# Moving the exponential ahead of a top-16 search, and cutting an MLP's second sum in two, in a four-layer transformer kernel

## The chip, the cores and the metric

The kernel runs on one core of a Trainium2 chip, as one program with one launch. The metric is the device time of the execution in microseconds (us); smaller is better. Engines are named as in the profile: PE (TensorE, matmul), DVE (VectorE), ACT (ScalarE), POOL (GpSimd) and SP (SyncE, which issues the DMAs).

## The reference

The input x has 128 sequences of 64 tokens with 128 features, in fp32; a context of the same shape and one condition vector per sequence come with it. Four layers follow each other, all with 16 heads of 8 features:

```python
x = L0(x)   # x + cross-attention(norm(x), norm(context))
x = L1(x)   # self-attention, cross-attention, GELU MLP; each with a residual
x = L2(x)   # self-attention, top-16 cross-attention, SwiGLU MLP
x = L3(x)   # self-attention, cross-attention, GELU MLP
```

The norms are scaled and shifted, and most residuals gated, by vectors made from the condition. The attention that the change touches is the second one of L2. There each query looks at 64 keys, and only the 16 with the greatest scores enter the softmax:

```python
scores = jnp.einsum('bqhd,bkhd->bhqk', q, k) / jnp.sqrt(jnp.float32(D))
top_s, top_i = jax.lax.top_k(scores, TOPK)          # TOPK = 16 of 64
attn = jax.nn.softmax(top_s, axis=-1)
vg = jnp.take_along_axis(v_bh[:, :, None, :, :], top_i[..., None], axis=3)
o = jnp.einsum('bhqk,bhqkd->bqhd', attn, vg)
```

In all there are 128 x 16 x 64 = 131072 such rows of 64 scores. Each MLP goes from 128 features to 512 and back; its second matmul is a sum over 4 blocks of 128.

## The kernel before

**Chunks and lanes.** The work is cut in 16 chunks of 8 sequences, that is 512 tokens; a chunk goes through all four layers before its result is stored. `network(LANES, False, acc)` runs eight lanes: eight chunks are in flight at once, each on a lane, and a lane takes the next chunk when its own is nearly written out.

**The order is planned while the program is built.** Every step is handed to `op(engine, cost, outs, ins, give, ...)`, with a cost in ns. `Plan.run` keeps a list of the lanes' next steps (a window of 80 for each), and takes again and again the one that could start earliest by its costs; this order is then the order of the instructions on each engine. `LUCK` is a tuple of 21 numbers, one for each 350 choices, which shift the costs by up to 1% and so break ties. Buffers are planned too: three PSUM tiles "mm" for projections and sums, two "ps" for scores, one "po", 30 SBUF tiles "some", and so on. Ahead of a PE step that the plan expects to idle for more than 1 us, `warm` (L1221) puts matmuls without use that fill half of the idle time.

**Attention.** `attention` makes k (L761, copied by ACT at L763), q (L767, copied with its bias at L770), spread over four row groups by four DMAs (L774), and v (L785, L792). Heads and sequences are then done in two "quads" of four sequences.

- In the plain attentions `weigh` makes the scores transposed (L819), ACT takes the exponential straight out of PSUM (L830), and no maximum is subtracted.
- In the top-16 attention `weigh_rows` makes the scores with queries on partitions (L849), one PSUM tile of 128 x 1024 for each of four steps. Each half of it (8 rows of 64 on each partition) is copied out by ACT (L867). DVE searches it, row by row: the 8 greatest (L887), these replaced by a very small number (L889), the next 8 greatest (L891). L902 then makes a mask of ones and zeros, `score >= 16th greatest`, and sums it up on its way, as `accum_out`, into `counts`. ACT takes the exponential of the scores (L909), POOL multiplies by the mask (L917), PE transposes (L925) and ACT copies to the probability tile (L934).
- `gather` multiplies with the values (L949), where two more columns of ones give the sums of the softmax; ACT copies the result (L959), and it is spilled to DRAM (L960). Sums and values are read back (L977, L981), DVE takes the reciprocal (L984), which is written (L986) and read back spread (L990), and POOL scales (L994). `project` (L1059) and `residual` (L1042, or L1046 and L1047 with a gate) end the attention.

**Norm and MLP.** A norm is L706 on DVE, L719 and L720 on POOL, L727 on DVE, a transpose on PE (L694), and scale and shift at L738 (DVE) and L739 (POOL), or a copy at L748. The MLPs are `gelu_mlp` and `swiglu_mlp` (first products at L1081), and end in `mlp_out`: 16 matmuls into one PSUM tile (L1072), 4 for each of 4 blocks of columns, given to the plan as one step.

**The guard.** Along with each attention POOL adds the reciprocals, the softmax sums and `counts` into three accumulators (L1007, L1008, L1012). After the last chunk these are compared with bounds, and the counts with an exact number; where one partition fails, a second network runs:

```python
nc.vector.tensor_scalar(ok[:, 8 * NH :], acc[2], float(8 * TOPK * nchunk), None, ALU.is_equal)
...
with tc.If(rows_ok < P):
    network(1, True)
```

This "safe" network does all 16 chunks over from the input, with one lane and few buffers (one for q, two for probabilities, ten "some"). All its attentions go through `weigh_rows`; in the plain ones DVE takes each row's maximum from PSUM (L870) and subtracts it (L871) ahead of the exponential, and in the top-16 one the 16 greatest are marked by two replacements, by place, and not by a comparison.

Of the kernel before, what the change touches and what calls it, by code (L numbers as in the profile page):

```python
# [10 lines left out]
AF = mybir.ActivationFunctionType  # L11
# [10 lines left out]
NT = T // P  # L22
# [4 lines left out]
LANES = 8  # L27
NJ = MLP // P
LUCK = (
    47423, 97277, 61821, 98454, 87219, 72030, 46625, 79421, 30261, 36474, 64224,  # L30
    16425, 63569, 65745, 68055, 16097, 89257, 63092, 89779, 79691, 72039,
)
NSOME = 30
NQBD, NPROB, NVAL = 3, 8, 4
SCALE = 1.0 / math.sqrt(HD)
# [64 lines left out]
PE, DVE, ACT, POOL, SP, LATER = "PE", "DVE", "ACT", "POOL", "SP", "LATER"  # L100
# [31 lines left out]
class Plan:  # L132
# [46 lines left out]
    def op(self, engine, cost, outs, ins, give, latency=0.0, bulk=False, table=None, small=0, within=False, port=False, moves=None, rate=1.0, code=4):  # L179
        tiles = list(dict.fromkeys([*outs, *ins]))  # L180
        needs = {}
        for t in tiles:
            if t.writer is not None:
                needs[t.writer] = True
        for t in outs:
            needs.update(dict.fromkeys(t.readers))
        o = Operation(engine, cost, latency, tiles, needs, give, bulk, table, small, within, port)
        o.moves, o.rate, o.code = moves, rate, small or code
        self.count += 1
        o.serial = self.count  # L190
        o.ev = 0 if engine == PE or any(t.kind in self.PSUM for t in tiles) else 1
        for t in outs:
            t.writer, t.readers = o, []
        for t in ins:
            if t not in outs:
                t.readers.append(o)
        for t in tiles:
            t.ops.append(o)
        self.ops.append(o)
# [180 lines left out]
def kernel(ctx: ExitStack, tc: tile.TileContext, ins: dict, out: bass.AP, nchunk: int = NCHUNK):  # L380
    nc = tc.nc
# [261 lines left out]
    def lane(n, plan, work, safe, acc, pieces, vblocks, queries, pool, spills):  # L643
# [4 lines left out]
        op = plan.op  # L648

        def of(*names):  # L650

            return [t for name in names for t in pieces.get(name, ())]

        def sb(shape, tag, bufs=1):
            name = f"{tag}{n}"
            return plan.tile(lambda: work.tile(shape, F32, tag=name, name=name, bufs=bufs), name, bufs)

        def mm(name):
            return plan.tile(lambda: mm_tile(name), "mm")
# [5 lines left out]
        def some(shape):  # L665


            def make():
                a = pool[t.slot]
                return a.rearrange("p (a b) -> p a b", a=shape[1]) if len(shape) == 3 else (  # L670
                    a.rearrange("p (a b c) -> p a b c", a=shape[1], b=shape[2]) if len(shape) == 4 else a
                )

            t = plan.tile(make, "some")
            return t
# [77 lines left out]
        def attention(hq, hkv, wq, bq, wk, wv, made, topk=False):  # L753
# [82 lines left out]
            def weigh_rows(i, prs):  # L836

                quad, gp = divmod(i, 2)
                psc = plan.tile(lambda: ps_s.tile([P, 2, 2, 2, 2, S], F32, tag="ps", name="ps"), "ps")
# [20 lines left out]
                for half in range(2):  # L860
                    ex = some([P, 8, S])

                    def s8(half=half):
                        return psc().rearrange("p g u k b s -> p (g u k b) s")[:, 8 * half : 8 * half + 8]

                    if topk:
                        op(ACT, 585, [ex], [psc], lambda ex=ex, s8=s8: nc.scalar.copy(ex(), s8()))  # L867
                    else:
                        mx = sb([P, 8], "mx", 2)
                        op(DVE, 680, [mx], [psc], lambda mx=mx, s8=s8: nc.vector.tensor_reduce(mx(), s8(), AX.X, ALU.max))  # L870
                        op(DVE, 680, [ex], [psc, mx], lambda ex=ex, mx=mx, s8=s8: nc.vector.tensor_tensor(  # L871
                            ex(), s8(), mx().unsqueeze(2).to_broadcast([P, 8, S]), ALU.subtract
                        ))
                    exs.append(ex)
# [31 lines left out]
                            ), port=True)  # L906
                        ws.append(w)
                for half, ex in enumerate(exs):
                    op(ACT, 570, [ex], [ex], lambda ex=ex: nc.scalar.activation(ex(), ex(), AF.Exp, scale=SCALE), table="exp")  # L909
                    if topk:  # L910
                        w = ws[half]
                        if safe:
                            op(DVE, 690, [ex], [ex, w], lambda ex=ex, w=w: nc.vector.scalar_tensor_tensor(
                                ex(), w(), GONE, ex(), ALU.is_equal, ALU.mult
                            ))
                        else:
                            op(POOL, 1255, [ex], [ex, w], lambda ex=ex, w=w: nc.gpsimd.tensor_tensor(  # L917
                                ex(), ex(), w(), ALU.mult
                            ), port=True)
# [45 lines left out]
            for quad in range(2):  # L965
                if topk or safe:
                    prs = probs()
                    for gp in range(2):
                        weigh_rows(2 * quad + gp, prs)
                else:  # L970
                    prs = weigh(quad)
                gather(quad, prs)
# [67 lines left out]
        def residual(py, x, gate, c, behind):  # L1040
            if isinstance(gate, str):
                op(DVE, 670, [x], [x, py], lambda: nc.vector.tensor_tensor(x(), v3(py()), x(), ALU.add))  # L1042
            else:
                g = by_token(gate, 0, c, [behind])
                y = some([P, NT, D])
                op(DVE, 650, [y], [py, g], lambda: nc.vector.tensor_tensor(y(), v3(py()), g(), ALU.mult))  # L1046
                op(POOL, 1255, [x], [x, y], lambda: nc.gpsimd.tensor_tensor(x(), x(), y(), ALU.add), port=True)  # L1047
# [16 lines left out]
        def mlp_out(gs, w2, x, gate, c):  # L1064

            py = mm("py")

            def sum_up():
                for t in range(NT):
                    cols = slice(t * P, (t + 1) * P)  # L1070
                    for j in range(NJ):
                        nc.tensor.matmul(  # L1072
                            py()[:, cols], lhsT=gs[j // 2]()[:, j % 2, cols], rhs=W[w2][:, j, :], start=(j == 0), stop=(j == NJ - 1)
                        )

            op(PE, 3610, [py], [*gs, *of(w2)], sum_up, code=4 * NT * NJ)
            residual(py, x, gate, c, gs[1])

        def product(w, j, h, name, *takes):
# [6 lines left out]
        def gelu_mlp(h, w1, b1, w2, x, gate, c):  # L1086
            gs = [shared([P, NJ // 2, T], "prob") for _ in range(2)]

            def part(j):
                ph = product(w1, j, h, "ph", *([] if j else gs))  # L1090
                op(ACT, 690, [gs[j // 2]], [ph, *of("biases")], lambda: nc.scalar.activation(
                    gs[j // 2]()[:, j % 2, :], ph(), AF.Gelu_apprx_tanh, bias=bvec(b1, j)
                ), table="gelu")

            for j in range(NJ):
                part(j)
            mlp_out(gs, w2, x, gate, c)

        def swiglu_mlp(h, w1, b1, w2, x, gate, c):

            gs = [shared([P, NJ // 2, T], "prob") for _ in range(2)]

            def part(j):
                pa = product(w1, j, h, "pa", *([] if j else gs))
                z = some([P, T])
                op(ACT, 690, [z], [pa], lambda: nc.scalar.activation(
                    z(), pa(), AF.Silu, bias=bvec(b1, j)
                ), table="silu")
                pg = product(w1, NJ + j, h, "pg")
                op(DVE, 740, [gs[j // 2]], [pg, z], lambda: nc.vector.scalar_tensor_tensor(  # L1110
                    gs[j // 2]()[:, j % 2, :], pg(), bvec(b1, NJ + j), z(), ALU.add, ALU.mult
                ))

            for j in range(NJ):
                part(j)
            mlp_out(gs, w2, x, gate, c)
# [187 lines left out]
```

## Time and profile before

| | |
|---|---|
| median of the runs | 1746.65 us (three: 1745.80, 1746.65, 1761.59) |
| the profiled execution, its own time | 1752.81 us |
| its span, first to last instruction | 1751.0 us |
| mean granted PE clock | 0.979 |
| instructions | 74746 |
| DMA, mean | 149 GB/s, 260.86 MB |

The page has the busy time of each engine and its share of the span, then groups of instructions by line: count, busy time, mean ns of one, and the idle time of the engine ahead of them with what ended it. In a timeline each line is the start and the length in us, the engine, the line of the kernel, the tiles written and read, and in brackets the idle time before it and who ended it. "PEld" is the loading of weights for a matmul. Line numbers are those of the kernel before.

### The profile page before, as it was taken

Reading aid. Unit: us, or ns where it says so; the run is one execution under the profiler, and the core shown is the slowest. Engines: PE = TensorE matmul, PEld = TensorE weight load, DVE = VectorE, ACT = ScalarE, POOL = GpSimd, SP = SyncE. Lnnn points to the kernel's source line nnn. Section 1 sums busy time; section 2 is a strip of 40 time slices with the busy share of each in tenths; the row PEclk is TensorE's granted clock in tenths of the full one; section 3 lists DMA queues with packets and bytes.
Section 4 is the critical chain, followed back from the end, with each engine's and each line's share of the span. In section 5 each row is a group of like instructions: output and inputs, shape, how many; then the busy total and the mean of one; then the engine's idle time right before and its main releaser. Section 6 shows DMA issues by size and latency. Waiting matters only on the chain. (4 is left out here: it accounts for less than half of the span.)

```text
span 1751.0 us, 74746 instructions
## 1 busy us (share of the span) xinstructions
PE 1624.2 (93%) x30425; PEld 1138.2 (65%) x30425; DVE 1248.4 (71%) x6009; ACT 1272.1 (73%) x1806; POOL 1117.3 (64%) x1306
## 2 busy tenths in 40 slices
PE   8977999988899999999998999999998999999998
PEld 5655667666566566766766666677676756666665
DVE  7532545699998976694578379399989899985323
ACT  3745777867587686788687859879887668686762
POOL 8642656666566757675766485586868566666444
PEclk9988999999999999999999999999999899999999
DMA  7576655543334456545654645755454325356343
GB/s 215 164 231 178 189 169 160 158 120 112 92 118 137 115 150 193 147 137 151 171 161 129 184 130 143 211 147 158 125 175 128 98 77 177 108 153 187 118 144 99
DMA packets 296821, 260.86 MB, mean 149 GB/s; under 512 B 53196, under 2 KB 216212, under 8 KB 296468
## 3 DMA queue, kind: packets, MB, share of 16 engines
q1 hardware_dynamic: 296468, 255.99, 50.2%
q8 instruction: 242, 3.96, 1.0%
q14 instruction: 111, 0.91, 0.2%
HBM read 154.83 MB, written 79.04 MB: 134 GB/s over the span
## 5 line engine op out<-in xcount | busy, mean ns | idle before, releaser
L830 ACT ACTIVATE prob<-ps 128x1024 f32<-128x1024 f32 x384 | 376.5, 1025 | 115.1 <-PE ps L819 112.7
L949 PEld LDWEIGHTS po<-prob,vbuf 128*32 128x32 f32 x14336 | 216.1, 111 | 89.1 <-issue 41.0
L949 PE MATMUL po<-prob,vbuf 128*32 128x64 f32 x14336 | 255.9, 223 | 9.6 <-issue 5.1
L727 DVE TENSOR_SCALAR some<-x,parts,rstd 128x128 f32<-128x128 f32 x640 | 212.4, 393 | 65.0 <-POOL rstd L720 64.8
L819 PE MATMUL ps<-qbd,some 32*64 32x256 f32 x6144 | 226.8, 393 | 18.8 <-DMA qbd<-some 14.1
L917 POOL TENSOR_TENSOR some<-some,some 128x512 f32<-128x512 f32 x128 | 163.6, 1286 | 102.7 <-ACT some L909 66.8
L720 POOL TENSOR_TENSOR rstd<-rstd,minus_half 128x4 f32<-128x4 f32 x192 | 199.0, 1037 | 16.0
L889 DVE MATCH_REPLACE8 some<-m,some 128x64 f32<-128x64 f32 x1024 | 206.4, 209 | 0.3 <-issue 0.3
L1047 POOL TENSOR_TENSOR x<-x,some 128x512 f32<-128x512 f32 x112 | 142.8, 1278 | 81.4 <-DVE some L1046 51.2
L994 POOL TENSOR_TENSOR some<-some,some 128x512 f32<-128x512 f32 x112 | 143.4, 1281 | 80.1 <-DMA some<-spillrec 20.9
L959 ACT COPY some<-po 128x512 f32<-128x512 f32 x224 | 132.6, 592 | 77.9 <-PE po L949 64.9
L887 DVE MAX8 m<-some 128x8 f32<-128x64 f32 x1024 | 172.1, 209 | 15.9 <-ACT some L867 15.9
L891 DVE MAX8 m<-some 128x8 f32<-128x64 f32 x1024 | 176.9, 214 | 0.0
L819 PEld LDWEIGHTS ps<-qbd,some 32*64 32x64 f32 x6144 | 119.7, 133 | 83.8 <-issue 41.0
L792 ACT COPY vbuf<-pv 64x512 f32<-64x512 f32 x224 | 154.2, 688 | 27.4 <-PE pv L785 25.3
L739 POOL TENSOR_TENSOR some<-some,mod_L 128x512 f32<-128x512 f32 x112 | 116.7, 1044 | 84.3 <-DVE some L738 62.5
L1038 POOL TENSOR_TENSOR x<-x,some 128x512 f32<-128x512 f32 x112 | 142.9, 1278 | 42.8 <-DVE some L727 26.5
L1046 DVE TENSOR_TENSOR some<-py,some 128x512 f32<-128x512 f32 x112 | 76.1, 683 | 115.8 <-PE py L1059 63.2
L706 DVE BATCH_NORM_STATS2 parts<-x 128x6 f32<-128x256 f32 x320 | 119.7, 418 | 34.9 <-POOL x L1047 34.0
L694 PE MATMUL pn<-ident,some 128*128 128x128 f32 x768 | 122.0, 283 | 7.2 <-DVE some L727 4.7
L694 PEld LDWEIGHTS pn<-ident,some 128*128 128x128 f32 x768 | 89.2, 142 | 51.1 <-issue 16.7
L763 ACT COPY some<-pk 128x512 f32<-128x512 f32 x112 | 66.3, 593 | 57.4 <-PE pk L761 46.5
(202 smaller groups left out, 3252.4 us busy)
## 6 DMA issues: line engine op xcount, KB each, us to landing
spill<-some SPq DMA_DIRECT2D x224, 256.0 KB, 3.4
some<-gates SPq DMA_DIRECT2D x224, 256.0 KB, 3.7
qbd<-some SPq DMA_DIRECT2D x448, 64.0 KB, 2.4
some<-spill SPq DMA_DIRECT2D x112, 256.0 KB, 4.0
some<-spillrec SPq DMA_DIRECT2D x112, 256.0 KB, 4.5
some<-in_ctx_dram SPq DMA_DIRECT2D x48, 256.0 KB, 5.1
gates<-once SPq DMA_DIRECT2D x7, 1024.0 KB, 7.4
x<-in_x_dram SPq DMA_DIRECT2D x16, 256.0 KB, 4.5
```

Of the source, the lines that this page charges most:

```text
L694: nc.tensor.transpose(p()[:, t * P : (t + 1) * P], x()[:, t, :], ident)
L720: nc.gpsimd.tensor_tensor(rstd(), rstd(), minus_half, ALU.pow)
L727: nc.vector.tensor_scalar(xn()[:, t, :], x()[:, t, :], mv()[:, t, 1:2], rstd()[:, t : t + 1], ALU.subtract, ALU.mult)
L792: nc.scalar.copy(v4(vbuf())[rows, :, :, 0 : 2 * HD].rearrange("p m h (d b) -> p m h d b", b=2)[:, :, :, :, b], pv()[rows].rearrange("p (m ...
L819: nc.tensor.matmul(pscs[g // 2]()[b * S : (b + 1) * S, g % 2, u].rearrange("p (h q) -> p h q", h=4), lhsT=kT()[rows, cols], rhs=qbd()[rows ...
L830: op(ACT, 975, [pr], [psc], lambda pr=pr, psc=psc: nc.scalar.activation(pr().rearrange("p g u h q -> p (g u h q)"), psc().rearrange("p g u ...
L887: nc.vector.max(m1()[:, j, :], ex()[:, j, :])
L889: nc.vector.match_replace(w()[:, j, :], m1()[:, j, :], ex()[:, j, :], GONE)
L891: nc.vector.max(m2()[:, j, :], w()[:, j, :])
L917: op(POOL, 1255, [ex], [ex, w], lambda ex=ex, w=w: nc.gpsimd.tensor_tensor(ex(), ex(), w(), ALU.mult), port=True)
L949: nc.tensor.matmul(po()[32 * j : 32 * j + 32, g, u], lhsT=vbuf()[:, at : at + 32], rhs=prs[gp]()[:, gi, u, j], start=True, stop=True,)
L994: nc.gpsimd.tensor_tensor(oT().rearrange("p (t b q) -> p b t q", b=2, q=S), oS().rearrange("p (b t q) -> p b t q", b=2, q=S), rb().rearran ...
```

## The change

In the fast network's top-16 attention, ACT no longer copies the scores out of PSUM but writes their exponentials, scaled by 1/sqrt(8) as before. The search, the mask and the counts work on these exponentials, and the exponential after the search goes. The safe network keeps its copy and its later exponential. The second sum of the MLPs is given to the plan as two steps of two column blocks each, the second of which may be taken as soon as the first is (`within`). `LUCK` has other numbers, and so the whole order is planned anew. Nothing else is different; the guard is the same.

```diff
 LUCK = (
-    47423, 97277, 61821, 98454, 87219, 72030, 46625, 79421, 30261, 36474, 64224,
...
+    69399, 87246, 10362, 72724, 8023, 6195, 73002, 47238, 78098, 36278, 14865,
...
                     if topk:
-                        op(ACT, 585, [ex], [psc], lambda ex=ex, s8=s8: nc.scalar.copy(ex(), s8()))
+                        if safe:
+                            op(ACT, 585, [ex], [psc], lambda ex=ex, s8=s8: nc.scalar.copy(ex(), s8()))
+                        else:
+                            op(ACT, 585, [ex], [psc], lambda ex=ex, s8=s8: nc.scalar.activation(
+                                ex(), s8(), AF.Exp, scale=SCALE
+                            ), table="exp")
...
-                    op(ACT, 570, [ex], [ex], lambda ex=ex: nc.scalar.activation(ex(), ex(), AF.Exp, scale=SCALE), table="exp")
+                    if safe or not topk:
+                        op(ACT, 570, [ex], [ex], lambda ex=ex: nc.scalar.activation(ex(), ex(), AF.Exp, scale=SCALE), table="exp")
...
-            def sum_up():
-                for t in range(NT):
+            def sum_up(half):
+                for t in (2 * half, 2 * half + 1):
...
-            op(PE, 3610, [py], [*gs, *of(w2)], sum_up, code=4 * NT * NJ)
+            for half in range(2):
+                op(PE, 1805, [py], [*gs, *of(w2)], lambda half=half: sum_up(half), code=2 * NT * NJ, within=half > 0)
             residual(py, x, gate, c, gs[1])
```

More of the change, by code (lines that the diff above doesn't have):

```diff
@@ L29 @@
 LUCK = (
-    47423, 97277, 61821, 98454, 87219, 72030, 46625, 79421, 30261, 36474, 64224,
-    16425, 63569, 65745, 68055, 16097, 89257, 63092, 89779, 79691, 72039,
+    69399, 87246, 10362, 72724, 8023, 6195, 73002, 47238, 78098, 36278, 14865,
+    98366, 49360, 99431, 12108, 19091, 99886, 63837, 50118, 9215, 3383,
 )
```

## The prediction

> **What bounds the kernel now.** I read the first line and part 1 of the page, then its groups, then the timeline of the last 60 us. The engines' shares say who is full:
>
> ```profile
> span 1751.0 us, 74746 instructions
> PE 1624.2 (93%) x30425; PEld 1138.2 (65%) x30425; DVE 1248.4 (71%) x6009; ACT 1272.1 (73%) x1806; POOL 1117.3 (64%) x1306
> L917 POOL TENSOR_TENSOR some<-some,some 128x512 f32<-128x512 f32 x128 | 163.6, 1286 | 102.7 <-ACT some L909 66.8 <-DVE m L887 22.9 <-DVE some L902 5.0
> L889 DVE MATCH_REPLACE8 some<-m,some 128x64 f32<-128x64 f32 x1024 | 206.4, 209 | 0.3 <-issue 0.3
> L867 ACT COPY some<-ps 128x512 f32<-128x512 f32 x128 | 69.7, 594 | 19.9 <-PE ps L849 15.7 <-issue 2.1 <-ACT some L867 0.9
> L909 ACT ACTIVATE some<-some 128x512 f32<-128x512 f32 x128 | 80.1, 638 | 15.1 <-DVE some L902 14.5
> ```
>
> PE is busy 93%, so what the change can win in the fast network is part of PE's idle 1751.0 - 1624.2 = 127 us. The 30425 PE records are the fast network alone: the guarded second network holds more PE work than the first, and none of it is in this span. That network is what my forecast turns on.
>
> **The change in the fast network.** Removed: 128 exponentials (L909), 80.1 us of ACT. The 128 PSUM copies (L867, 594 ns) become exponentials: by the row of L909 638 ns, so 128 x 44 ns = 5.6 us back. Table loads, counted in the two programs: 106 before, 100 after, at 1283 ns (the loads of L830, 38.5 us for 30): 7.7 us less. ACT falls by about 82 us, but it is 73% busy beside PE. One wait is added: the search (L887) now stands behind an exponential, which may stand behind a table load (7 of the 100 do, 9 us in all); queued behind it on DVE are norms and residuals, covered by DVE's 29% of idle time, at worst 9 us. What can reach PE: PE waited for L917, the mask product, in its row for the transposes L925 (36.4 us in the load row, 18.1 us in the matmul row). L917's largest idle (66.8 us) waits for L909, which goes; next late is the mask L902 on DVE, whose exponentials are then already there. Bounds: 0 and 54 us; as most of L917's wait is POOL's and not PE's, I take 15. The halves of the MLP sums issue the same 1536 matmuls; their bounds are a few us either way (a smaller job for the planner to place; an op of 1.1 us slipped between the halves delays the residual L1046 by that much). The planner's new numbers reorder everything: +-10 us. With the 1.8 us that the profiled execution has around its span, the fast network comes to 1752.8 - 15 = 1738. The median shown (1746.65) is 0.4% under the profiled execution; I leave that in the range.
>
> **What the guard sees.** The mask L902 counts scores that are >= the 16th greatest, and the end of the program compares the counts with exactly 16 per row. Equal values at places 16 and 17 give 17, and then the whole safe network runs. Until now the values compared were scores. I evaluated the reference in fp32, with its inputs, up to L2's cross-attention: 128 x 16 x 64 = 131072 rows. The scaled score at place 16 has a median size of 0.029 and is positive in 86% of the rows; the gap to place 17 has a median of 0.00136. As scores, the spacing of fp32 there is some 2e-9: the expected number of rows with a tie is 0.1, and the trace without a second network agrees. As exponentials the values lie around 1.03, where fp32 is spaced 1.2e-7 apart. 725 rows have the two exponentials within 100 spacings, 73 within 10, 8 within one; a pair closer than one spacing rounds to one value with a chance that falls linearly from 1 to 0, so 725 / 100 / 2 = 3.6 rows tie. Moving all scores at random by a few 1e-8 moves which rows, not how many: 1 to 8 in ten draws. No tie at all has a chance of exp(-3.6) = 2.7%. [...] With an exponential of unlimited resolution the sum would be 1738 us; with that rounding the safe network is added. No value shows in a trace; I take the rounding.
>
> **The price of the safe network.** It runs one lane: one chunk after the other, 16 times, with single buffers, so its time is a chain of latencies. The tail of the trace, where the last lane is nearly alone, has that chain (ACT's bias copy of q, scores, spill, reciprocal, scaling, residual, norm):
>
> ```profile
> 1694.05 0.69 ACT L770 ACTIVATE some<-pq,mixed_bias 128x512 f32<-128x512 f32 x1 [0.40 <-PE pq L767]
> 1698.90 0.66 PEld L819 LDWEIGHTS ps<-qbd,some 32*64 32x64 f32 x32
> 1710.36 0.37 SPq L960 DMA_DIRECT2D spill<-some  x1
> 1723.40 1.27 POOL L994 TENSOR_TENSOR some<-some,some 128x512 f32<-128x512 f32 x1 [1.28 <-DVE some L727]
> 1726.91 0.69 DVE L1042 TENSOR_TENSOR x<-py,x 128x512 f32<-128x512 f32 x1
> 1727.64 0.76 DVE L706 BATCH_NORM_STATS2 parts<-x 128x6 f32<-128x256 f32 x2
> 1733.19 1.04 POOL L739 TENSOR_TENSOR some<-some,mod_L 128x512 f32<-128x512 f32 x1
> ```
>
> Starts to ends: q copied to scores begun 4.2 us (four DMAs); spill issued to scaling done 14.3, of which some 0.8 is a wait for DVE's port: 13.5; projection and residual 2.05 (1.05 PE, 0.69 DVE, hops of about 0.15); norm to modulated h 6.6 here and 5.8 one lane earlier: 5.9, or 4.7 where a copy on ACT takes the modulation's place; k and q for h 3.1 in self-attention, 2.0 in cross; a gated residual's POOL add 1.4.
> Between scores and spill the safe network does other work: in a plain attention, for each half of a score tile, a row maximum and a subtraction on DVE, then exponential, transposes, copy. The maximum from PSUM is in no row; the nearest, DVE's 128x512 reads of PSUM (L738, 682 ns), bounds it at 0.5 to 0.8, and I take 0.68. Both quads use the same two probability tiles, so the second's scores wait for the first's gather. One quad: scores 1.2, DVE 8 x 0.68 = 5.4, exponential 0.64, transposes 0.64, copy 0.6, half a gather 0.65, hops 0.8: 9.9. Two: 20, and 0.75 for the last copy.
> Plain attention: 4.2 + 20 + 0.75 + 13.5 + 2.05 = 40.5 from q on. With norm, k and q and gate, L0: 49.5; the three self-attentions 50.9 each; L1c and L3c 47.2 each. In the top-k attention the search is on the path: per row L887, L889 with its load, L891 and a second match are 172.1 + 2 x (206.4 + 84.1) + 176.9 us over 1024 = 0.91 us; 8 rows 7.3, mask 0.8, wait for POOL's subtraction 0.4: 8.5 per half, 8 halves and some 9 us around them: 77 instead of 20, so 106.8. The seven: 403.
> A GELU MLP: norm 5.9, products and activations 4.4, sum 3.6, residual 2.2: 16.1, two of them; SwiGLU 20; output stored and next x loaded 6.3. Sum: 403 + 32 + 20 + 6 = 461 us a chunk.
>
> **The clock.** [...] Start to start of the warming matmuls' loads:
>
> ```profile
> 2.50 0.33 PEld L1221 LDWEIGHTS ph<-ident 128*128 128x128 f32 x1 [0.52 <-issue]
> 3.36 0.33 PEld L1221 LDWEIGHTS ph<-ident 128*128 128x128 f32 x1 [0.52 <-issue]
> 7.66 0.19 PEld L1221 LDWEIGHTS pb<-ident 128*128 128x128 f32 x1 [0.24 <-issue]
> 8.10 0.19 PEld L1221 LDWEIGHTS pb<-ident 128*128 128x128 f32 x1 [0.24 <-issue]
> ```
>
> 0.86 us cold, 0.44 warm. The fast network's mean granted clock is 0.979, and by it nothing is to be added. [...] I take 30, and 9 for instructions in each other's way: 500 us a chunk.
> 16 x 500 = 8000. With 12 us for the guard, the branch and clearing buffers: 1738 + 8000 + 12 = **9750 us**.
>
> **Rivals.**
> A. The safe network overlaps more than a chain. Its fullest engine is DVE: per chunk 65 in the search, 66 in six softmaxes, about 40 in norms and residuals: 170 us, 2.7 ms in all, total 4.5 ms. One lane with one x tile speaks against it. In the other direction, PE cold throughout and DMAs as slow as under load give 560 a chunk: 10700.
> B. No row ties (the other side): 1738 us, 0.5% under the median: for it only the luck of 2.7%. With all of the 54 us 1700.
> C. No tie, and the new order costs: exponentials ahead of the search keep a score buffer until a table is loaded, and the second half of a sum holds one of three PSUM buffers longer. If each of the 48 sums puts a 1.1 us op in PE's way: +53, 1791 us. It decides from the 14th on, which eats up the 15 us gained.
>
> **Numbers.** Forecast 0.95 (with A's two directions 0.15 of it outside the range), B 0.04 (half of it over 1% faster, half within), C 0.01. A measurement of this kernel tells about 1% from no change. 9750 +- 10% is what the chain's unknowns make (the maximum at 0.5 to 0.8, 768 times on the chain: -138 to +92; clock -480 to +500; spill to scaling +- 2 us, 112 times: 224): 8800 to 10800.
>
> **What would show it.** Right: a span of some 9.7 ms, PE well under half busy after 1.74 ms, rows of the row maximum (none before), match-replaces 3072 instead of 1024, granted clock well under 0.979 in the second part; per chunk about 500 us from output store to output store. Wrong: a span near 1740 without row maxima (the counts came out exact), or a second part of another length, whose spill-to-scaling and search stretches then say which term was off.

## The result, and the profile after

The changed kernel takes 8639.38 us, the median of four runs (8628.5 to 8651.83), against 1746.61 us for the kernel before: 4.937 times as long, with a 95% interval of 4.909 to 4.964. The second, guarded network runs, as forecast; the forecast of 9750 us and its range from 8800 were too high.

The first lines of the page of the changed kernel, its clock row, and two of its groups (columns: line, engine, operation, tiles, count | busy us, mean ns | idle us before, and who ended it):

```profile
span 8630.5 us, 213484 instructions
PE 7207.3 (84%) x89603; PEld 4405.1 (51%) x89603; DVE 3616.7 (42%) x15417; ACT 2994.4 (35%) x4616; POOL 2115.8 (25%) x2350
...
PEclk9999999999999999899999999999999998999999
DMA  6445554511111111111111111111111111111111
...
L1000 POOL TENSOR_TENSOR some<-some,some 128x512 f32<-128x512 f32 x224 | 285.4, 1275 | 3813.6 <-DMA some<-spillrec 2607.9
L875 DVE TENSOR_REDUCE mx<-ps 128x8 f32<-128x512 f32 x768 | 493.2, 684 | 1279.5 <-PE ps L849 1279.2
```

The instructions have almost tripled, the 768 row maxima (L875) exist only in the safe network, and the scaling L1000 (L994 before) ran 224 times, twice for each of 112 attentions. The DMA row drops from 4 to 6 tenths to 1 after the eighth slice: one lane is left. POOL waited 3813.6 us in front of L1000, 2607.9 of them for one DMA: a chain of latencies. PE's 84%, where I had forecast well under half in the second part, mislead: the page's rows of the warming matmuls (L1228) into the tiles ppt, pn and py alone are 945.5 + 791.5 + 583.1 = 2320 us of its 7207. And the clock row, where I had expected far less, stays at 8 to 9 tenths. The hand-over, in the timeline (start us, length us, engine, line):

```profile
1738.16 0.13 DVE L1281 CAST n_ok<-pok 1x1 int32<-1x1 f32 x1
1738.39 1.26 POOL L1053 TENSOR_TENSOR x<-x,some 128x512 f32<-128x512 f32 x1 [7.48 <-DVE n_ok L1281]
1739.08 5.78 PE L1228 MATMUL pn<-ident 128*128 128x512 f32 x14 [1.44 <-DVE n_ok L1281]
1739.68 0.38 SPq L1214 DMA_DIRECT2D out_dram<-x  x1
1742.19 0.39 SPq L683 DMA_DIRECT2D x<-in_x_dram  x1
```

The guard's number is ready at 1738.3 us, PE is in the safe network 0.8 us later, and the first chunk's x is fetched again at 1742.2. From there to 8630.5 are 6888 us, 430.5 for each of 16 chunks.

### The profile page after: what moved, and what is told of

The parts are those of the page before. It is cut to its first block, busy times and chain, and to the rows that moved or that the text cites. A ratio compares the mean times of both kernels' runs of the same rounds, so it can differ in the third digit from the quotient of the medians.

```text
span 8630.5 us, 213484 instructions
## 1 busy us (share of the span) xinstructions
PE 7207.3 (84%) x89603; PEld 4405.1 (51%) x89603; DVE 3616.7 (42%) x15417; ACT 2994.4 (35%) x4616; POOL 2115.8 (25%) x2350
## 5 line engine op out<-in xcount | busy, mean ns | idle before, releaser
L1000 POOL TENSOR_TENSOR some<-some,some 128x512 f32<-128x512 f32 x224 | 285.4, 1275 | 3813.6 <-DMA some<-spillrec 2607.9
L875 DVE TENSOR_REDUCE mx<-ps 128x8 f32<-128x512 f32 x768 | 493.2, 684 | 1279.5 <-PE ps L849 1279.2
L931 PE MATMUL ppt<-ident,some 128*128 128x128 f32 x4096 | 650.3, 294 | 446.5 <-DVE some L919 243.1
L1228 PE MATMUL ppt<-ident 128*128 128x512 f32 (+24 forms) x2174 | 945.5, 566 | 0.4 <-issue 0.4
L915 ACT ACTIVATE some<-some 128x512 f32<-128x512 f32 x896 | 536.9, 630 | 1040.9 <-DVE some L876 451.5
L1228 PE MATMUL pn<-ident 128*128 128x512 f32 (+14 forms) x1636 | 791.5, 633 | 1.4 <-DVE n_ok L1281 1.4
L940 ACT COPY prob<-ppt 128x512 f32<-128x512 f32 x1024 | 575.9, 587 | 445.7 <-PE ppt L931 441.8
L849 PE MATMUL ps<-some,qbd 32*64 32x64 f32 x32768 | 631.6, 223 | 97.4 <-DMA qbd<-some 66.7
L849 PEld LDWEIGHTS ps<-some,qbd 32*64 32x64 f32 x32768 | 548.5, 134 | 203.5 <-DMA qbd<-some 97.9
L1228 PEld LDWEIGHTS ppt<-ident 128*128 128x128 f32 x2174 | 407.1, 205 | 360.5 <-issue 348.9
L1228 PE MATMUL py<-ident 128*128 128x512 f32 (+10 forms) x1418 | 583.1, 560 | 0.0
L1228 PEld LDWEIGHTS pn<-ident 128*128 128x128 f32 x1636 | 344.8, 222 | 374.9 <-issue 373.4
L876 DVE TENSOR_TENSOR some<-ps,mx 128x512 f32<-128x512 f32 x768 | 491.1, 681 | 0.0
```

Of the source, the lines that this page charges most:

```text
L849: nc.tensor.matmul(psc()[e * S : (e + 1) * S, gi, u, k, b], lhsT=qbd()[rows, 2 * k + e, cols], rhs=kT()[rows, cols], start=True, stop=True,)
L931: nc.tensor.transpose(ppt()[:, k * P : (k + 1) * P], ex()[:, 2 * k : 2 * k + 2, :].rearrange("p b s -> p (b s)"), ident,)
L940: nc.scalar.copy(pr8[:, 4 * half : 4 * half + 4], ppt().rearrange("p (k q) -> p k q", k=4))
L1000: nc.gpsimd.tensor_tensor(oT().rearrange("p (t b q) -> p b t q", b=2, q=S), oS().rearrange("p (b t q) -> p b t q", b=2, q=S), rb().rearran ...
L1228: nc.tensor.matmul(flat[:, :n], lhsT=ident, rhs=ident[:, 0:1].to_broadcast([P, n]), start=True, stop=True)
```

## Experiments: is it the ties?

Five kernels ask what starts the second network. Edits are cut to the lines, or parts of lines, that matter.

**e1** takes the second network out of the question by muting the guard:

```diff
-    with tc.If(rows_ok < P):
+    with tc.If(rows_ok < 1):
```

> The changed kernel with one number different: the second network runs only if no partition passes the guard, instead of if one fails. It leaves the second network out where a few rows tie. Theory (ties start the safe network, which is all of the added time): the time falls from 8639 to the fast network's own, 1738 by the prediction, 1735 to 1745 by the changed kernel's profile, in which the last store of the fast network is issued at 1739.7 us. Rival 1 (the new order or the moved exponentials slow the fast network itself): clearly over 1747. Rival 2 (more than ties is wrong with the counts, so that every partition fails): still about 8640.

Measured: 1752.81 us (12 runs) beside 1748.91 for the kernel before; ratio 1.0015, interval 0.9997 to 1.0032. At least one partition passes, so the counts are not wrong everywhere, and all of the added 6.9 ms is the second network. Without it the changed kernel can't be told from the kernel before; that it would take 1735 to 1745 us was a miss, and no gain is left of the forecast 15 us.

**e2** counts the extra places, with branches in place of the guard:

```diff
+    for k in range(12):
+        with tc.If(some_more > k):
+            nc.gpsimd.memset(acc[1], float(k))
```

> The changed kernel's fast network, and in place of the guard and the second network a sum of the counts less 16 per row over all 131072 rows, followed by twelve branches, the k-th taken if the sum is over k; each taken branch runs one memset of 128 x 64. It leaves the safe network out. Theory (rounding of the exponentials): 3.6 rows expected, so 1 to 8 memsets, most likely 3 or 4. Rival (the exponential as this engine computes it is coarser than fp32, or equal values are replaced together in the search): all twelve. Rival (another reason for the second network): none. Time 1740 to 1760 with the branches.

Its timeline at the end, POOL alone:

```profile
1736.38 1.26 POOL L1053 TENSOR_TENSOR x<-x,some 128x512 f32<-128x512 f32 x1 [7.48 <-DVE n_more L1279]
1737.58 0.36 POOL L1283 MEMSET sumsum<- 128x64 f32 x2
```

Two memsets: the counts of 131072 rows hold 2 places too many, that is two tied rows, or one with two extra places. Two places cost 6.9 ms.

**e8** is the kernel before, with no exponential in the comparison; it puts the scores where fp32 is coarse:

```diff
-lambda ex=ex, s8=s8: nc.scalar.copy(ex(), s8())
+lambda ex=ex, s8=s8: nc.scalar.copy(ex(), s8()) if safe else nc.scalar.activation(
+    ex(), s8(), AF.Identity, bias=sixteen, scale=SCALE)
```

> The fast network of the kernel before, where ACT copies the scores out of PSUM as scale * score + 16 instead of as they are (the exponential later takes them as they are; a factor of e to the 16th cancels in the softmax). No exponential is in the comparison. In place of the guard, branches at 0, 1, 2, 4, 8, 16, 32, 40, 48, 56, 64, 72, 80, 96, 128 and 256 extra places, one memset of 128 x 64 for each that is passed. It leaves the safe network out. Theory (only the spacing of fp32 where the compared values lie counts): at 16 it is 1.9e-6, 16 times that at 1, and the reference's scores give 55 to 61 rows; with a scatter of 8: 8 to 11 memsets. Rival (it is something about the exponential): 0.

```profile
1739.62 1.35 POOL L1280 MEMSET sumsum<- 128x64 f32 x6
1741.33 0.89 POOL L1280 MEMSET sumsum<- 128x64 f32 x4 [0.37 <-POOL sumsum L1280]
```

Ten memsets: more than 56 and at most 64 extra places, where 55 to 61 had been worked out. The kernel before, which compares scores, has none (its second network never runs); with 2 around 1 and 57 to 64 at 16 the number follows the spacing of fp32 at the compared values. The exponential matters only by putting values of about 0.03 at about 1.03.

**e3** starts the safe network in the kernel before, by a number that the counts can't meet:

```diff
-float(8 * TOPK * nchunk), None, ALU.is_equal
+float(8 * TOPK * nchunk + 1), None, ALU.is_equal
```

> The kernel before, with the guard's number raised by one, so that it always fails and the safe network always runs. Theory (the added time is the safe network, and nothing of the change is in it): 8639 within 1%, that is 1747 + 6888. Rival (the changed kernel's second part is slowed by what the change did to its order): shorter by more than 1%.

Measured: 8666.99 us, once; 0.3% over the changed kernel. The safe network takes as long behind either fast network, within that 0.3%.

**e4** is the changed kernel, but searches scores again and takes the exponentials from the same PSUM tile beside the copy:

```diff
+op(ACT, 585, [ex], [psc], lambda ex=ex, s8=s8: nc.scalar.copy(ex(), s8()))
+if not safe:
+    op(ACT, 585, [pr], [psc], lambda half=half, s8=s8: nc.scalar.activation(
+        parked(half), s8(), AF.Exp, scale=SCALE), table="exp")
...
-ex(), ex(), w(), ALU.mult
+ex(), parked(half), w(), ALU.mult
```

> The changed kernel, with scores searched again: ACT copies the scores out of PSUM for the search, the mask and the counts, and takes the exponentials out of the same PSUM tile as well, parked in the probability tile; POOL multiplies those with the mask. ACT does as much as before the change, POOL no longer waits for an exponential after the mask. Theory (the exponent as the thing compared starts the second network): no second network, 1735 to 1755, within 1% of the kernel before. Rival (the second network starts for another reason, such as the new order): about 8640.

Measured: 1859.38 us, ratio 1.0625 (1.0601 to 1.0649). The second network does not run, as the theory says; the exponentials are the same as in the changed kernel, and of what the guard looks at only the comparison differs, so it is the comparison of exponentials that starts it. That it is 6% slower than the kernel before was a miss. It has planner numbers of another program, which is taken up below; it also holds the score tile for two readers, and which of the two costs the 6% was not tried. No version here beats the kernel before.

## Experiments: why the safe network is shorter than reckoned

**e5** leaves the warming matmuls out of the forced safe network:

```diff
 def warm(tile, ns):
+    if safe:
+        return
```

> The forced kernel (the one before, with a guard that always fails), with the warming matmuls left out of the safe network. PE work on the chain per chunk, at the warm rate: 9.7 us in each of 7 attentions (projection 1.05, transposes of the norm 0.6, k and q 2.1, first scores 1.2, per quad scores, transposes and half a gather 2.35) and some 5 in each of 3 MLPs, 83 us. Theory (the warming matmuls keep the clock up; that is why the clock term of 30 us a chunk was too large): the granted clock falls to 0.5 to 0.6 in the second part and the time rises by up to 16 x 83 = 1330 us, to 9700 to 10000. Rival (the clock doesn't matter on this chain, or the useless matmuls stand in the way themselves): within 1% of 8667, or under it.

Measured: 9253.49 us, 586 more than e3, 37 for each chunk (e5 to e7 ran once each, on another chip than e3; the kernel before takes 1755.18 us there and 1748.91 on e3's). Busy time in a stretch of the second part (its length, then PE, PEld, DVE, ACT and POOL with their instructions, then granted clock, DMA share and GB/s); first e3:

```profile
1745.00:8300.00 6555.00, 5324.09 (x56145) 3110.43 (x56144) 2248.28 (x8865) 1698.98 (x2788) 951.54 (x994) 0.92 0.13 36
```

and e5:

```profile
1745.00:8300.00 6555.00, 3152.36 (x45212) 2351.06 (x45212) 2076.77 (x8238) 1585.43 (x2571) 876.25 (x916) 0.60 0.12 33
```

The clock falls from 0.92 to 0.60, and PE's busy share from 81% to 48%, so that only without the warming matmuls PE comes near the forecast's "well under half". So the warming works: placed at the front of a wait, it still carried the clock across most of what I had counted as lost (the mean matmul record of q is 1.14 us here and 0.74 in the changed kernel, where the kernel before has 0.62). Of the 37 us a chunk, by the two traces, 24 lie between the copy of q and the second spill of the seven attentions and 13 in all the rest. It is worth less than the bound of 1330 us, because PE is not slow throughout without it. The scores of one attention's two quads in e5:

```profile
2756.31 4.12 PE L849 MATMUL ps<-some,qbd 32*64 32x64 f32 x124 [0.27 <-DMA qbd<-some]
2768.66 2.56 PE L849 MATMUL ps<-some,qbd 32*64 32x64 f32 x128
```

The first quad's 124 score matmuls take 4.12 us, the second's 128 only 2.56.

**e6** gives the safe network four probability tiles:

```diff
-"prob": 2 if safe else NPROB
+"prob": 4 if safe else NPROB
```

> The forced kernel with four probability tiles in the safe network instead of two, so that the second quad's scores need not wait for the first quad's gather. Theory (the two quads of an attention stand one after the other on the chain, 8.98 us each, of which DVE works 5.2): up to 3.7 us less for each of 96 plain attentions and somewhat less for the 16 top-16 ones, 300 to 420 us, to 8250 to 8370. Rival (ten SBUF tiles hold the quads apart anyway): 8620 to 8700.

Measured: 8306.89 us, 360 less than e3. The quads do stand one behind the other on the chain, as the prediction had them.

**e7** leaves out the second replacement of the safe search:

```diff
-for j in rows if safe else ():
-    nc.vector.match_replace(w()[:, j, :], m2()[:, j, :], w()[:, j, :], GONE)
```

> The forced kernel with the second replacement (a load and a replacement for each of 64 rows a partition, 16 times) left out of the safe network's search; the eight places it would mark stay unmarked. Theory 1 (as the prediction reckoned, by the durations of the records: 206.3 + 83.0 us over 1024 rows): 289 us less than 8667. Theory 2 (the records overlap; from start to start the pair of replacements takes 0.38 us for two rows): 0.19 x 1024 = 195 us less. Rival (the search is hidden behind other work): no change.

Measured: 8505.74 us, 161 less than e3. The 289 that the records' busy times give are out; it is nearer to 195, from start to start, and somewhat under it. The rest is a wait that the replacement had hidden. After each half of a score tile (four steps of two rows) DVE waits for POOL's subtraction (L897, L895 in e7); first e3, then e7:

```profile
2843.42 0.35 DVE L887 MAX8 m<-some 128x8 f32<-128x64 f32 x2 [0.59 <-POOL some L897]
2825.98 0.35 DVE L887 MAX8 m<-some 128x8 f32<-128x64 f32 x2 [0.97 <-POOL some L895]
```

In all DVE waits 56.7 us for it in e3 and 93.7 in e7, 37 more, and 195 - 37 = 158. The DVE timeline of the changed kernel shows why durations mislead (one pair of rows, then the start of the next):

```profile
3706.29 0.35 DVE L892 MAX8 m<-some 128x8 f32<-128x64 f32 x2 [8.52 <-ACT some L868]
3706.57 0.08 DVE L894 MATCH_VALUE_LOAD some<-m,some 128x8 f32 x1
3706.63 0.21 DVE L894 MATCH_REPLACE8 some<-m,some 128x64 f32<-128x64 f32 x1
3706.76 0.08 DVE L894 MATCH_VALUE_LOAD some<-m,some 128x8 f32 x1
3706.83 0.21 DVE L894 MATCH_REPLACE8 some<-m,some 128x64 f32<-128x64 f32 x1
3706.95 0.35 DVE L896 MAX8 m<-some 128x8 f32<-128x64 f32 x2
3707.22 0.08 DVE L898 MATCH_VALUE_LOAD some<-m,some 128x8 f32 x1
3707.28 0.21 DVE L898 MATCH_REPLACE8 some<-m,some 128x64 f32<-128x64 f32 x1
3707.41 0.08 DVE L898 MATCH_VALUE_LOAD some<-m,some 128x8 f32 x1
3707.48 0.21 DVE L898 MATCH_REPLACE8 some<-m,some 128x64 f32<-128x64 f32 x1
3707.60 0.34 DVE L892 MAX8 m<-some 128x8 f32<-128x64 f32 x2
```

A replacement of 0.21 us is overtaken by the next load after 0.13. Two rows take 1.31 us, 0.65 each, where the prediction's sum of busy times says 0.91.

## Experiments: where the gain of the fast network went

Four kernels split the change; in e9 and e12 the guard is muted as in e1. The edits of e9, e10 and e11 are shown against the kernel before, that of e12 against the changed kernel.

**e9**: the exponentials out of PSUM alone.

```diff
-op(ACT, 585, [ex], [psc], lambda ex=ex, s8=s8: nc.scalar.copy(ex(), s8()))
+op(ACT, 585, [ex], [psc], lambda ex=ex, s8=s8: nc.scalar.activation(ex(), s8(), AF.Exp, scale=SCALE), table="exp")
```

> The kernel before with the exponentials out of PSUM alone: the planner's old numbers, sums in one piece, and the guard muted as in e1 (the second network is left out where a few rows tie). Theory (ACT's 82 us were off the path and the product's wait passes from the exponential to the mask): ratio 0.99 to 1.01. Rival (the change gains its 15 us and the new numbers take it back): 0.991 or less here, and e11 over 1.005.

**e10**: the sums in halves alone.

```diff
-op(PE, 3610, [py], [*gs, *of(w2)], sum_up, code=4 * NT * NJ)
+for half in range(2):
+    op(PE, 1805, [py], [*gs, *of(w2)], lambda half=half: sum_up(half), code=2 * NT * NJ, within=half > 0)
```

> The kernel before with the MLPs' second sums in two halves alone, old numbers, scores searched. Theory (the same 1536 matmuls, placed a little differently): ratio 0.99 to 1.01. Rival (an op between the halves holds back the residuals): up to 1.03.

**e11**: the planner's numbers alone.

```diff
-    47423, 97277, 61821, ...
+    69399, 87246, 10362, ...
```

> The kernel before with the changed kernel's planner numbers alone, so another order of the same work. Theory (numbers that fit one program are no better than any for another): 1.00 to 1.03, over what e9 and e10 show. Rival (the numbers matter less than 0.5%): 0.995 to 1.005.

**e12**: both edits with the old numbers.

```diff
-    69399, 87246, 10362, ...
+    47423, 97277, 61821, ...
```

> The changed kernel with the planner's old numbers and the muted guard: exponentials out of PSUM and sums in halves. Theory (numbers are fitted to the program they came with): slower than e1's 1.0015, 1.005 to 1.04. Rival (numbers do not matter): 1.0015 within 0.005.

| | ratio to before | interval |
|---|---|---|
| e1, all three | 1.0015 | 0.9997 to 1.0032 |
| e9, exponentials | 1.0334 | 1.0311 to 1.0357 |
| e10, halves | 1.0479 | 1.0457 to 1.0500 |
| e11, numbers | 1.0205 | 1.0178 to 1.0231 |
| e12, exponentials and halves | 1.0501 | 1.0475 to 1.0528 |

I had expected 0.99 to 1.01 for e9 and e10, and both missed. e1 and e12 are one program with different numbers: 1.0501 / 1.0015 is 4.9%, some 85 us, from the numbers alone; e11 and the kernel before are one program too, 2% apart. Each program with numbers that came with another one is 2 to 6% slower, e4 with them. In e4, e9 and e10 an edit and unfit numbers come together, so the edit itself may have a part in it. The parts can't be valued one by one in this way: what each edit is worth with numbers fitted to it was not tried. What stands is that the three together come to nothing.

The wait that the edit removed passed on. In e1 PE's busy time and the product's row (L923, L917 before) are:

```profile
span 1746.7 us, 74728 instructions
PE 1622.8 (93%) x30429; PEld 1135.6 (65%) x30429; DVE 1238.7 (71%) x6009; ACT 1200.8 (69%) x1672; POOL 1116.1 (64%) x1306
...
L923 POOL TENSOR_TENSOR some<-some,some 128x512 f32<-128x512 f32 x128 | 162.7, 1274 | 96.7 <-DVE some L907 57.5
```

The exponential, 66.8 us of idle time before, is gone from it, and the mask (L907, L902 before) now ends 57.5 us in its place; 102.7 us of idle time became 96.7. PE's waits for the product fell from 54.5 to 43.4 us, but all of PE's idle time only from 126.8 (1751.0 - 1624.2) to 123.9 (one profiled execution each): most of it came back in front of other work.

## Why the prediction was right and wrong

**What the guard sees: right.** The step held with the size in the count (3.6 worked out, 2 measured; 55 to 61 and 57 to 64 at 16), and two places were enough. Rival B and its 2.7% are excluded for this kernel by its own page, C's 53 us by e1. Rival A's overlap doesn't hold: DVE, its fullest engine, is busy 2248 of 6555 us in e3's second part.

**The fast network: wrong by 15 us.** ACT's busy time fell by 71.3 us (1272.1 to 1200.8 in e1) where 82 were reckoned, and the ratio is 1.0015. The step that failed is the choice of 15 us between 0 and 54: it should have been 0. PE did wait 11 us less for the product, since the mask, which I named as next late, ends 57.5 us of POOL's idle time where it had ended 5.0; but a wait taken away in front of PE is not time taken off the span, and PE's idle time fell by 3. Which of the three edits brought the rest back is not shown. The +-10 us for the planner's numbers was an undersized term: by e1 and e12 they can move some 85 us.

**The price of the safe network: right in kind, 70 us of 500 a chunk too long.** That is the step that put the forecast out of its range: the sum of the chain was mis-sized. DMA issues in the changed kernel, SP alone, with which its stretches can be read off in one chunk:

```profile
3481.85 0.38 SPq L1214 DMA_DIRECT2D out_dram<-x  x1
...
3494.86 2.43 SPq L774 DMA_DIRECT2D qbd<-some  x4
3508.14 9.29 SPq L966 DMA_DIRECT2D spill<-some  x2
...
3700.99 2.42 SPq L774 DMA_DIRECT2D qbd<-some  x4
3735.72 31.25 SPq L966 DMA_DIRECT2D spill<-some  x2
...
3911.22 0.38 SPq L1214 DMA_DIRECT2D out_dram<-x  x1
```

From store to store 429.4 us. A row of two spills lasts from the first's start to the second's end, so a plain quad takes 9.29 less the second's 0.36: 8.93. From the first query DMA to the first spill a plain attention takes 13.3 us and the top-16 one 34.7, with 30.9 for its second quad.

The trace of the changed kernel gives the same for all chunks. Cut at the end of q's copy (L770), at the second spill (L966), at the end of the scaling (L1000) and at the store, chunks 2 to 16 have these means:

| stretch, us a chunk | predicted | measured | difference |
|---|---|---|---|
| q copied to second spill, six plain attentions | 148.5 (4.2 + 2 x 9.9 + 0.75 each) | 138.3 (23.04 each) | -10.2 |
| the same, top-16 attention | 82.0 (4.2 + 77 + 0.75) | 66.2 | -15.7 |
| spill to scaling done, seven times | 94.5 (13.5 each) | 83.5 (11.93 each) | -11.0 |
| all the rest: projections, residuals, norms, k and q, MLPs, store and load | 136 | 142 | +6 |
| the clock | 30 | in the rows above | -30 |
| instructions in each other's way | 9 | in the rows above | -9 |
| sum | 500 | 430 | -70 |

So 37 of the 70 us lie in stretches that were reckoned too long, and 33 in additions of 39 of which the rest of the chain shows 6. The terms that make the difference:

- *The search* was summed up from the busy times of the page's rows (0.91 us a row); from start to start a row takes 0.65, and 64 rows a partition make 16.4 us of it. The timeline of the kernel before shows the same overlap: there a step of two rows, without the second replacement, takes 0.92 us, where the busy times give 1.25.

```profile
1502.36 0.34 DVE L887 MAX8 m<-some 128x8 f32<-128x64 f32 x2
...
1503.28 0.33 DVE L887 MAX8 m<-some 128x8 f32<-128x64 f32 x2
```

This term I had taken as certain and given no range.
- *The quads.* Row maximum and subtraction overlap on DVE too. In the changed kernel two of one kind and two of the other start 1.20 us apart, 0.60 for each, where 0.68 was taken:

```profile
3499.56 1.29 DVE L875 TENSOR_REDUCE mx<-ps 128x8 f32<-128x512 f32 x2 [7.89 <-PE ps L849]
...
3500.77 1.28 DVE L876 TENSOR_TENSOR some<-ps,mx 128x512 f32<-128x512 f32 x2
...
3501.97 1.28 DVE L875 TENSOR_REDUCE mx<-ps 128x8 f32<-128x512 f32 x2
```

For eight that is 0.6 us a quad; a quad takes 9.1 on average where 9.9 was reckoned.
- *Spill to scaling* was read in the tail of the kernel before, where some lanes still moved data and POOL waited 1.28 us for DVE, an order that the program itself sets (`port in turn`). With nothing else on the queues the scaling starts 1789.90 - 1779.63 = 10.3 us after the spill is issued and takes 1.3; where loads of gates or context are issued ahead of the last read it takes up to 12.6 on average. The range had this term at +-2 us, and the mean used 1.6 of that.
- *The clock.* The 30 us a chunk were an estimate of mine, and no run shows them. What the runs showed in their place is a loss that lies mostly in the projection, the first PE work after the longest wait; here with 4.17 us of idle time in front of it:

```profile
1789.90 1.26 POOL L1000 TENSOR_TENSOR some<-some,some 128x512 f32<-128x512 f32 x1 [35.33 <-DMA some<-spillrec]
1791.21 2.08 PE L1065 MATMUL py<-w_L_xcond_Wp,some 128*128 128x128 f32 x8 [4.17 <-POOL some L1000]
```

It takes 2.08 us, where the kernel before has 1.05 (L1059, at 1710.14 us); over the second part of the changed kernel the mean is 1.77 (198.6 us of PE for 112 projections). The work that follows is nearer to the rate of the kernel before than to that of e5, without warming. Mean matmul records:

| us | kernel before | changed kernel, second part | e5 |
|---|---|---|---|
| projection | 0.28 | 0.39 | 0.44 |
| q | 0.62 | 0.74 | 1.14 |
| k of the self-attentions | 0.62 to 0.63 | 0.65 to 0.77 | 1.14 |
| the norm's transposes | 0.28 | 0.34 | 0.45 |
| scores (L849) | 0.22 | 0.22 | 0.28 |

By these numbers the projection loses 0.7 us in each attention, the two matmuls of q 0.24, the four transposes 0.2, and the two matmuls of k 0.15 in a self-attention, some 9 us a chunk in all; that is an estimate, of the size of the 6 us in the table above. The clock of 0.92 against the 0.60 without warming points the same way. The mean granted clock of the kernel before (0.979), by which nothing was to be added, would have been the better choice here.

One term is misread besides: by its sum L0 was given 3.1 us for k and q, the self-attention's figure, instead of 2.0 for cross-attention; that is 18 us in all.

**The range.** Of its three unknowns the row maximum has records of 684 ns, as taken, but costs 0.60 us; the clock's 30 us were nearly void; spill to scaling was 1.6 us too long. The search had no range. The errors went one way because busy times were added up that overlap, because one latency was read with other work in its way, and because two additions on top were hardly needed. A range made of terms with either sign doesn't hold such a sum.

## What to carry to other kernels

A function put in front of a comparison changes how many values are equal: ask what the spacing of the number format is where the function puts them, and multiply by the number of rows before taking a case for impossible. Where a guard starts a second path, its price belongs to every edit that touches what the guard looks at. A gain on an engine that is off the critical path is worth what the next late input leaves of it (here 102.7 us of POOL's idle time became 96.7), and in a planned order the plan's fit can outweigh the edit (4.9% between e1 and e12). What a repeated step costs is read in the trace from start to start, and not summed from its records (1.31 us for two rows of the search, where the busy times add up to 1.82).

## What the runs showed of the hardware

- On DVE successive small instructions overlap: a replacement recorded with 0.21 us is followed by the next load after 0.13 us, and a search step of two rows takes 1.31 us where the lines of its four MAX8, four loads and four replacements add up to 1.86 (changed kernel, 3706.29 us). The busy times of the second replacement are 289 us; leaving it out saved 161 (e7 against e3), with 37 us more of waiting for POOL.
- With warming matmuls at the front of PE's waits (8.16 of the 12.33 us from 1778.88 us of the changed kernel to its projection) the mean granted clock was 0.92 (e3, 1745 to 8300 us); without them it was 0.60 on the same chain (e5), and the run took 9253 us, 586 more than e3. Behind the wait named the projection still took 2.08 us, where the kernel before has 1.05; its mean in the second part was 1.77.
